# Two matrix products change places, and a bias addition moves from GpSimd to VectorE, in a two-layer graph attention kernel

## The chip, the cores and the metric

The kernel runs on one core of one Trainium2 chip. The metric is the device time of one execution in microseconds (us). The engines are named as in the profile: PE (TensorE, the matrix unit; PEld is its loading of weights), DVE (VectorE), ACT (ScalarE), POOL (GpSimd) and SP (SyncE, which here only issues DMA transfers). Each engine works through its own queue in order; between engines, semaphores hold an instruction back until what it needs is done.

## The reference

There are 64 graphs of 256 nodes with 512 features each, all in float32. Two layers follow each other, each with a residual connection and a normalization over the features:

```python
# layer 0: graph attention, 8 heads of 64
feats = einsum('bnf,hfu->bhnu', X, W)
dense = leaky_relu(e_self[..., :, None] + e_neigh[..., None, :], 0.2)
att = softmax(dense + NEG_BIG * (1 - A))
out = relu(einsum('bhij,bhju->bhiu', att, feats) + b)
x = layernorm(x + out)
# layer 1: attention with an adjacency and a distance term, 8 heads of 64
q, k, v = split(x @ W_qkv)
attn = softmax(q @ k.T / 8) * 0.33 + 0.33 * adj + 0.33 * exp(-adj)     # masked
x = layernorm(x + (attn @ v) @ W_out + b_out)
```

## The kernel before

The nodes of a graph lie in two tiles of 128 rows (`T` = 2) and the features in four chunks of 128 (`C` = 4). The loop runs over the graphs `b`, and one turn of it works on four graphs at once, at different stages: layer 0's attention for graph b (`attend0`), layer 1's projections for b-1 (`proj1`), layer 1's scores for b-1 and its weighting and output for b-2 (`softmax1`, `attend1`), and layer 0's projection for b+1 (`proj0`). A turn is `attention0_beside_projections1(b)` followed by `attention1_beside_projections0(b)`. Both are lists of `do(stage, graph, step, ...)` calls, and `in_order()` ties every instruction to the one issued before it on its engine. So the order of these calls is the order of every engine's queue; no scheduler changes it.

**Seven products for eight.** The projections are multiplied as 2 by 2 blocks in Strassen's manner: seven products p1 to p7, in three PSUM banks. The bank "chain" takes p1, p6, p7 and p4, each added to what lies in the bank; after each of them ACT copies the running sum out (line 301). The bank "alone" takes p2. The bank "pair" takes p5 and then p3. DVE makes the remaining blocks from a bank and one of ACT's copies: `add 11` reads "alone", `add 22` reads "pair" when it holds p5, `add 12` reads "pair" when it holds p5 + p3 (line 304).

```python
BANK = dict(p1="chain", p6="chain", p7="chain", p4="chain", p2="alone", p5="pair", p3="pair")
FIRST = ("p1", "p2", "p5")
COPIES = dict(p1=11, p6=12, p7=22, p4=21)
ADDED = {11: "alone", 22: "pair", 12: "pair"}
```

Two waits follow from this. A product of "chain" waits until ACT has copied the one before it out of the bank, and p3 waits until `add 22` has read the bank. Line 292 holds the matrix products of all three users: `pq_p` (q and k of layer 1), `pv_p` (v of layer 1) and `pf_p` (the features of layer 0, with two columns per head for the attention's logits). All PSUM tiles of this kind rotate through four buffers (`ps_tile`).

**Around the end of the first list.** The second half of v's block ends with p4, the last product of layer 0's attention (`attend0 product 1, 1`, line 539), p3 and `add 12`. Then come `end` (two DVE operations, line 563, which add the input x and sum the rows), the features of the next graph, and between them `squares` of layer 0's normalization on ACT (line 343), the weights of layer 1 (`weights 2` and `weights 3`: two DVE operations each, line 750 times the inverse row sums, line 757 plus the adjacency term), and `norm`. The normalization itself is a chain over three engines: DVE sums (563), POOL takes the mean (338), ACT the squares (343), POOL the factors (350, 353, 354: `shift`), ACT applies them (358). ACT also makes `far`, `at` and `mf` (lines 384, 385, 387) out of the transposed adjacency `adjT` (DVE, line 121) just ahead of the features' first copy. In the second list, the score products `pz` (line 668) use two buffers of their own; ACT's exponentials (line 677) free them.

**The output bias.** `residual` (line 820) adds `b_out`, spread over all rows, to the layer's input `X1[b]` before `sum_up` (line 780) adds the projected attention to it. It has two instructions per graph on POOL (line 822) and stands at the end of the first list, for graph b-2.

**The start of the first list.** Here the products of q and k run between layer 0's weights (`attend0 weights`, line 520, DVE), which begin with `nd` (line 443); `nd` waits for `gb`, a row that is written to DRAM and read back to all partitions. `qk_add 11` and `qk_add 22` are the DVE additions of q and k (line 304).

Of the kernel before, what the change touches and what calls it, by code (L numbers as in the profile page):

```python
# [17 lines left out]
def kernel(  # L18
# [29 lines left out]
    nc = tc.nc  # L48
    P = 128
    NB, N, F = x.shape  # L50
    H, _, U = w0.shape
    T = N // P
# [22 lines left out]
    def ps_tile(shape, name):  # L75

        return psum.tile(shape, FT, tag="mm", name=name, bufs=4)
# [47 lines left out]
    def load(b):  # L125

        XB[b] = io.tile([P, C, N // B, B], FT, tag="xb", name=f"xb_{b}", bufs=1)
        load_blocks(XB[b], x[b])

    def load_adj(b):  # L130
        ADJB[b] = io.tile([P, T, N // B, B], FT, tag="adj", name=f"adj_{b}", bufs=1)
        load_blocks(ADJB[b], adj[b])
        MROW[b] = io.tile([P, N], U8, tag="mask", name=f"mask_{b}", bufs=4)
        nc.sync.dma_start(MROW[b], nodemask[b].partition_broadcast(P))
# [36 lines left out]
    bo_bc = consts.tile([P, F], FT, name="bo_bc")  # L171
# [340 lines left out]
    X1, NORM = {}, {}  # L512
# [231 lines left out]
    def attend1(b):  # L744
        oT = work.tile([P, C, N], FT, tag="oT", name=f"oT_{b}", bufs=1)
        av = {}

        def weights(g):
            p, k = PROBS[b][g], 2 * (g % 2)
            nc.vector.tensor_mul(  # L750
                p,
                p,
                REC[b][:, k : k + 2, g // 2, :]
                .unsqueeze(2)
                .to_broadcast([P, 2, T, N]),
            )
            nc.vector.tensor_add(  # L757
                p, p, CT[b].unsqueeze(1).to_broadcast([P, 2, T, N])
            )

        def values(g):

            if g % 2 == 0:
                av[0] = ps_tile([P, 2, N], f"av1_{b}_{g}")
            for j in range(T):
                for r in range(2):
                    matmul(  # L767
                        av[0][r * U : (r + 1) * U, g % 2, :],
                        V1[b][:, j, 2 * g + r, :],
                        PROBS[b][g][:, r, j, :],  # L770
                        start=(j == 0),
                        stop=(j == T - 1),
                    )
            if g % 2 == 1:
                nc.scalar.copy(oT[:, g - 1 : g + 1, :], av[0])

        def sum_up(po, t):
            if t == 0:
                NORM["l1", b] = LayerNorm(X1[b], b, "l1")
            nc.vector.scalar_tensor_tensor(  # L780
                X1[b][:, t, :],
                po,
                1.0,
                X1[b][:, t, :],
                op0=ALU.mult,
                op1=ALU.add,
                accum_out=NORM["l1", b].sums[:, t : t + 1],
            )
            if t == T - 1:
                NORM["l1", b].mean()  # L790

        PO = {}

        def values_project(g):

            pav = ps_tile([P, N], f"av1_{b}_{g}")
            for j in range(T):
                for r in range(2):
                    matmul(
                        pav[r * U : (r + 1) * U, :],  # L800
                        V1[b][:, j, 2 * g + r, :],
                        PROBS[b][g][:, r, j, :],
                        start=(j == 0),
                        stop=(j == T - 1),
                    )
            nc.scalar.copy(oT[:, g, :], pav)
            if g == 0:
                PO[0] = psum.tile([P, T, F], FT, tag="sc", name=f"po_{b}", bufs=2)
            for t in range(T):
                matmul(  # L810
                    PO[0][:, t, :],
                    oT[:, g, t * P : (t + 1) * P],
                    wo_sb[:, g, :],
                    start=(g == 0),
                    stop=(g == C - 1),
                )
                if g == C - 1:
                    sum_up(PO[0][:, t, :], t)

        def residual():  # L820
            for t in range(T):
                nc.gpsimd.tensor_add(X1[b][:, t, :], X1[b][:, t, :], bo_bc)

        def project(t):
            po = ps_tile([P, F], f"po_{b}_{t}")
            for c in range(C):
                matmul(  # L827
                    po,
                    oT[:, c, t * P : (t + 1) * P],
                    wo_sb[:, c, :],  # L830
                    start=(c == 0),
                    stop=(c == C - 1),
                )
            sum_up(po, t)

        def store():
            NORM.pop(("l1", b)).apply()
            nc.sync.dma_start(out[b].rearrange("(t p) f -> p t f", p=P), X1[b])

        return dict(  # L840
            weights=weights,
            residual=residual,
            values=values,
            values_project=values_project,
            project=project,
            squares=lambda: NORM["l1", b].squares(),
            store=store,
        )
# [3 lines left out]
        proj0=proj0, attend0=attend0, proj1=proj1, softmax1=softmax1, attend1=attend1  # L852
# [3 lines left out]
    def do(stage, b, step, *args):  # L856

        if 0 <= b < NB:
            if (stage, b) not in S:
                S[stage, b] = stages[stage](b)  # L860
            S[stage, b][step](*args)
            in_order()
# [13 lines left out]
    def attention0_beside_projections1(b):  # L876


        do("attend1", b - 3, "squares")
        do("proj1", b - 1, "qk", "p1")  # L880
        do("proj1", b - 1, "qk", "p2")
        if b > 0:
            do("proj0", b, "columns")
        do("proj1", b - 1, "qk", "p6")
        for h in range(HG):
            if b > 0:
                do("proj0", b, "scaled", h)
            do("attend0", b, "weights", h)
        do("attend1", b - 3, "store")
        do("proj1", b - 1, "qk_add", 11)  # L890
        do("proj1", b - 1, "qk", "p5")
        do("proj1", b - 1, "qk", "p7")
        do("proj1", b - 1, "qk_add", 22)
        do("attend0", b, "product", 0, 0)
        if b > 0:
            for h in range(HG, H):
                do("proj0", b, "scaled", h)
        do("proj1", b - 1, "qk", "p4")
        do("attend0", b, "product", 0, 1)
        do("attend1", b - 2, "weights", 0)  # L900
        for h in range(HG, H):
            do("attend0", b, "weights", h)
        do("attend0", b, "norm0", 0, 0)
        do("attend0", b, "norm0", 0, 1)
        do("proj1", b - 1, "qk", "p3")
        do("proj1", b - 1, "qk_add", 12)
        do("attend1", b - 2, "weights", 1)
        do("proj0", b + 1, "xT")
        if b + 2 < NB:
            load(b + 2)  # L910
        do("proj1", b - 1, "values", "p1")
        do("proj1", b - 1, "values", "p2")
        do("proj1", b - 1, "v_add", 11)
        do("proj1", b - 1, "values", "p6")
        do("proj1", b - 1, "values", "p5")
        do("proj1", b - 1, "values", "p7")
        do("proj1", b - 1, "v_add", 22)
        do("proj0", b + 1, "aT")
        if b + 2 < NB:
            load_adj(b + 2)  # L920
        do("attend0", b, "product", 1, 0)
        do("proj1", b - 1, "values", "p4")
        do("proj0", b + 1, "far")
        do("attend0", b, "product", 1, 1)
        do("attend0", b, "norm0", 1, 0)
        do("attend0", b, "norm0", 1, 1)
        do("proj1", b - 1, "values", "p3")
        do("proj1", b - 1, "v_add", 12)
        do("attend0", b, "end")
        do("proj0", b + 1, "product", "p1")  # L930
        do("proj0", b + 1, "product", "p2")
        do("proj0", b + 1, "add", 11)
        do("proj0", b + 1, "product", "p6")
        do("proj0", b + 1, "product", "p5")
        do("proj0", b + 1, "product", "p7")
        do("attend0", b, "squares")
        do("proj0", b + 1, "add", 22)
        do("attend1", b - 2, "weights", 2)
        do("proj0", b + 1, "product", "p4")
        do("attend0", b, "norm")  # L940
        do("proj1", b, "blocks")
        if b + 1 < NB:
            load_rows(b + 1)
        do("proj0", b + 1, "product", "p3")
        do("proj0", b + 1, "add", 12)
        do("attend1", b - 2, "weights", 3)
        do("attend1", b - 2, "residual")

    def attention1_beside_projections0(b):

# [138 lines left out]
```

## Time and profile before

| what | value |
| --- | --- |
| runs shown | 3252.85 us median of 4 (3251.99 to 3253.42) |
| the profiled execution: its time, and its span from first to last instruction | 3252.31 us, 3250.6 us |
| granted PE clock in it | 0.989 |
| busy: PE, DVE, ACT, POOL | 3148.1, 2693.2, 1463.6, 482.9 us |
| one turn of the loop (from one `po` group to the next, 1599.44 to 1648.62) | 49.18 us |
| line 822, POOL, 128x512 | 128 times, 1748 ns mean |
| line 750 / line 757, DVE, 128x1024 | 256 times each, 1217 / 1493 ns mean |
| line 465, DVE, 128x1056, one operand spread over rows | 63 times, 1252 ns mean |

Times are given from the start of the span. In the list of waits, a line names who waited, for whom, the sum in us, how often, and the longest. In the timeline, a line has the start and the length in us, engine, source line, operation, output and inputs, their shapes, the number of instructions merged into it, and in brackets how long the engine had been idle and what ended that. Ends of matrix products are modelled.

### The profile page before, as it was taken

What the parts mean: (1) busy time and instruction counts of PE and PEld (TensorE: products, weight loads), DVE (VectorE), ACT (ScalarE), POOL (GpSimd) and SP (SyncE); (2) the same over time, 40 slices, a digit from 0 to 9 for tenths busy, and PEclk for the clock granted to TensorE, in tenths of its full rate; (3) what the DMA queues carried; (4) which work ended last, traced back from release to release, by engine and by line L of the source; (5) the groups of instructions that cost most, each with busy time, mean ns of one, the idle gap of its engine ahead of it and who ended that gap; (6) DMA issues with size and microseconds to landing.
All of it is one profiled execution on the core that took longest, in us unless ns stands there. A gap on an engine that the chain in (4) does not pass through costs nothing.

```text
span 3250.6 us, 55684 instructions
## 1 busy us (share of the span) xinstructions
PE 3148.1 (97%) x21262; PEld 2491.9 (77%) x21262; DVE 2693.2 (83%) x5088; ACT 1463.6 (45%) x3585; POOL 482.9 (15%) x646
## 2 busy tenths in 40 slices
PE   4999999999999999999999999999999999999997
PEld 4877877877877878878778778778778778778774
DVE  6688888888888888888888888888888888888874
ACT  1344444454444444444444444444444544444442
POOL 0011111111111111111111111111111111111111
PEclk7999999999999999999999999999999999999998
DMA  7244343443443443443443443443444434434421
GB/s 156 68 115 97 102 115 92 106 115 88 108 112 88 108 114 87 109 107 94 112 105 93 115 99 99 115 93 106 115 92 105 115 87 109 111 88 110 112 70 51
DMA packets 764394, 331.87 MB, mean 102 GB/s; under 512 B 696672, under 2 KB 697440, under 8 KB 747744
## 3 DMA queue, kind: packets, MB, share of 16 engines
q1 hardware_dynamic: 764128, 328.30, 39.9%
q8 instruction: 169, 2.77, 0.3%
q14 instruction: 97, 0.79, 0.1%
HBM read 259.80 MB, written 68.16 MB: 101 GB/s over the span
## 4 chain that ended last, share of the span: by engine, by line
PE 95%; ACT 1%; DMA 1%; DVE 1%; SPq 1%; issue 0%; POOL 0%; ACTq 0%; DVEq 0%; POOLq 0%
PE pq_p L292 25%; PE av L539 14%; PE po L827 14%; PE pf_p L292 12%; PE pv_p L292 12%; PE pz L668 8%; PE av L767 7%; PE pd L697 2%; PE pr L82 1%; ACT v L301 1%; SPq L114 0%; PE po L810 0%; DMA hb<-hs 0%; DMA hs<-x 0%; DMA gb<-gs 0%
## 5 line engine op out<-in xcount | busy, mean ns | idle before, releaser
L539 PEld LDWEIGHTS av<-v,pT 128*128 128x128 f32 x4096 | 493.9, 194 | 19.1 <-ACT v L485 12.6
L539 PE MATMUL av<-v,pT 128*128 128x65 f32 x4096 | 491.7, 274 | 12.3 <-ACT v L485 12.3
L292 PE MATMUL pq_p<-hC,wqk_sb 128*128 128x128 f32 x4096 | 482.9, 276 | 0.9 <-ACT qk L301 0.9
L292 PEld LDWEIGHTS pq_p<-hC,wqk_sb 128*128 128x128 f32 x4096 | 467.9, 192 | 2.5 <-ACT qk L301 1.6
L827 PE MATMUL po<-wo_sb,oT 128*128 128x512 f32 x1008 | 460.6, 600 | 0.0
L520 DVE SCALAR_TENSOR_TENSOR pT<-gb,ccol,at 128x256 f32<-128x256 f32 x1024 | 416.9, 480 | 25.0 <-ACT ccol L448 17.8
L757 DVE TENSOR_TENSOR p<-p,ct 128x1024 f32<-128x1024 f32 x256 | 382.2, 1493 | 8.7
L292 PE MATMUL pq_p<-hT,wqk_sb 128*128 128x128 f32 x3072 | 378.0, 280 | 10.4 <-DVE hT L121 9.6
L292 PEld LDWEIGHTS pq_p<-hT,wqk_sb 128*128 128x128 f32 x3072 | 357.1, 194 | 37.1 <-DVE hC L270 25.1
L338 POOL TENSOR_SCALAR nmean_l<-sums_l 128x2 f32<-128x2 f32 x128 | 28.7, 224 | 2349.1 <-DVE x L563 1593.9
L301 ACT COPY v<-pv_p 128x256 f32<-128x256 f32 x256 | 95.3, 372 | 560.8 <-PE pv_p L292 560.8
L827 PEld LDWEIGHTS po<-wo_sb,oT 128*128 128x128 f32 x1008 | 182.0, 190 | 205.0 <-issue 203.6
L750 DVE TENSOR_TENSOR p<-p,rb 128x1024 f32<-128x1024 f32 x256 | 311.5, 1217 | 5.2 <-DMA rb<-rs 5.2
L677 ACT ACTIVATE p<-pz,hide 128x512 f32<-128x512 f32 x512 | 312.2, 708 | 3.3 <-PE pz L668 3.3
L343 ACT ACTIVATE junk<-x,nmean_l 128x512 bf16<-128x512 f32 x256 | 184.9, 722 | 267.8 <-POOL nmean_l L338 263.6
L668 PE MATMUL pz<-qk 64*128 64x256 f32 x2048 | 268.1, 399 | 4.9 <-ACT p L677 4.9
L358 ACT ACTIVATE x<-x,shift_l,rstd_l 128x512 f32<-128x512 f32 x256 | 193.7, 804 | 170.0 <-POOL shift_l L354 170.0
L485 ACT ACTIVATE v<-v 128x64 f32<-128x64 f32 x1024 | 258.6, 339 | 0.0
L767 PE MATMUL av<-p,v 128*64 128x256 f32 x2016 | 249.3, 389 | 2.7 <-DVE p L757 2.7
L668 PEld LDWEIGHTS pz<-qk 64*128 64x128 f32 x2048 | 184.1, 188 | 86.2 <-ACT p L677 46.1
L292 PE MATMUL pv_p<-wv_sb,hC 128*128 128x256 f32 x1024 | 245.5, 382 | 0.0
L292 PE MATMUL pf_p<-wf_sb,xC 128*128 128x264 f32 x1008 | 244.9, 386 | 0.0
(107 smaller groups left out, 4112.4 us busy)
## 6 DMA issues: line engine op xcount, KB each, us to landing
gb<-gs SPq DMA_DIRECT2D x64, 1028.0 KB
rb<-rs SPq DMA_DIRECT2D x64, 1024.0 KB, 4.5
x<-in_x_dram SPq DMA_DIRECT2D x64, 512.0 KB, 4.2
hs<-x SPq DMA_DIRECT2D x64, 512.0 KB
hb<-hs SPq DMA_DIRECT2D x256, 128.0 KB, 3.1
out_dram<-x SPq DMA_DIRECT2D x64, 512.0 KB, 2.9
xb<-in_x_dram SPq DMA_DIRECT2D x252, 128.0 KB, 3.7
adj<-in_adj_dram SPq DMA_DIRECT2D x256, 64.0 KB, 2.9
```

What stands on the lines that cost most here:

```text
L292: matmul(d, lhsT, rhs, start=(p in FIRST and i == 0), stop=(i == len(todo) - 1), skip_group_check=True,)
L343: nc.scalar.activation(junk, self.src[:, t, :], AF.Square, bias=self.nmean[:, t : t + 1], accum_out=self.rstd[:, t : t + 1],)
L358: nc.scalar.activation(self.src[:, t, :], self.src[:, t, :], AF.Identity, bias=self.shift[:, t : t + 1], scale=self.rstd[:, t : t + 1],)
L485: nc.scalar.activation(V0[b][:, t, h, :U], V0[b][:, t, h, :U], AF.Copy, scale=V0[b][:, t, h, U : U + 1],)
L520: nc.vector.scalar_tensor_tensor(pT[h][:, j, :], GB[b][:, h, :N], CCOL[b][:, j, h : h + 1], AT[b][:, j, :], op0=ALU.max, op1=ALU.mult,)
L539: matmul(av[:, k, :], pT[h][:, j, t * P : (t + 1) * P], V0[b][:, j, h, :UA], start=(j == 0), stop=(j == T - 1),)
L668: matmul(pz[:, r, j, :], QK[b][rows, g, 1, j * P : (j + 1) * P], QK[b][rows, g, 0, :], start=True, stop=True,)
L677: nc.scalar.activation(p[:, :, j, :], pz[:, :, j, :], AF.Exp, bias=hide[:, j, b : b + 1], scale=U**-0.5,)
L750: nc.vector.tensor_mul(p, p, REC[b][:, k : k + 2, g // 2, :] .unsqueeze(2) .to_broadcast([P, 2, T, N]),)
L757: nc.vector.tensor_add(p, p, CT[b].unsqueeze(1).to_broadcast([P, 2, T, N]))
L767: matmul(av[0][r * U : (r + 1) * U, g % 2, :], V1[b][:, j, 2 * g + r, :], PROBS[b][g][:, r, j, :], start=(j == 0), stop=(j == T - 1),)
L827: matmul(po, oT[:, c, t * P : (t + 1) * P], wo_sb[:, c, :], start=(c == 0), stop=(c == C - 1),)
```

## The change

`residual` becomes one DVE instruction over both row tiles in place of two POOL instructions. In the first list it moves from the end to the place between `qk_add 11` and `qk_add 22` of the same turn, for the same graph b-2. In the closing list `end()`, its two calls stand where they stood, and run on DVE. At the end of the first list, the features' p1 moves ahead of v's p3, and the features' p2 and `add 11` move behind p7.

```diff
         def residual():
-            for t in range(T):
-                nc.gpsimd.tensor_add(X1[b][:, t, :], X1[b][:, t, :], bo_bc)
+            nc.vector.tensor_add(
+                X1[b], X1[b], bo_bc.unsqueeze(1).to_broadcast([P, T, F])
+            )
...
         do("proj1", b - 1, "qk_add", 11)
         do("proj1", b - 1, "qk", "p5")
         do("proj1", b - 1, "qk", "p7")
+        do("attend1", b - 2, "residual")
         do("proj1", b - 1, "qk_add", 22)
...
         do("attend0", b, "norm0", 1, 1)
+        do("proj0", b + 1, "product", "p1")
         do("proj1", b - 1, "values", "p3")
         do("proj1", b - 1, "v_add", 12)
         do("attend0", b, "end")
-        do("proj0", b + 1, "product", "p1")
-        do("proj0", b + 1, "product", "p2")
-        do("proj0", b + 1, "add", 11)
         do("proj0", b + 1, "product", "p6")
         do("proj0", b + 1, "product", "p5")
         do("proj0", b + 1, "product", "p7")
+        do("proj0", b + 1, "product", "p2")
+        do("proj0", b + 1, "add", 11)
         do("attend0", b, "squares")
         do("proj0", b + 1, "add", 22)
...
         do("attend1", b - 2, "weights", 3)
-        do("attend1", b - 2, "residual")
```

## The prediction

> **What bounds the kernel now.** First the page: which engine sets the end.
>
> ```profile
> PE 95%; ACT 1%; DMA 1%; DVE 1%; SPq 1%; issue 0%; POOL 0%; ACTq 0%; DVEq 0%; POOLq 0%
> ```
>
> PE carries 95% of the chain that ended last. A change gains only where PE waits, and loses only where it makes PE wait. Next the list of waits, for the places that the change touches.
>
> ```profile
> DVE nd L443 <- DMA gb<-gs: 103.6, 64, 3.5
> DVE qk L304 <- ACT qk L301: 77.4, 63, 3.1
> ...
> PEld pz L668 <- ACT p L677: 46.1, 124, 3.4
> ...
> PE pf_p L292 <- ACT v L301: 29.5, 63, 0.5
> ```
>
> The last row is the wait that the new order takes away: p4 of the features waits for ACT's copy of p7. The second is the gap that is to hold the bias addition: DVE waits for the copy ahead of `qk_add 22`, 1.2 us in the mean. The third says that the scores, later in the same turn, wait for ACT too. Third, the timeline of one turn, engine by engine; I count from S = 1628.85, the start of v's p3, just behind layer 0's last attention product.
>
> ```profile
> 1634.85 1.16 PE L292 MATMUL pf_p<-wf_sb,xT 128*128 128x264 f32 x4 [0.47 <-ACT v L301]
> ```
>
> ```profile
> 1629.73 0.39 ACT L387 CAST mf<-mask 128x256 f32<-128x256 uint8 x1
> ...
> 1634.42 0.38 ACT L301 COPY v<-pf_p 128x264 f32<-128x264 f32 x1 [1.40 <-PE pf_p L292]
> ...
> 1639.22 1.52 ACT L358 ACTIVATE x<-x,shift_l,rstd_l 128x512 f32<-128x512 f32 x2 [2.60 <-POOL shift_l L354]
> ```
>
> ```profile
> 1636.44 1.27 POOL L350 TENSOR_SCALAR rstd_l<-rstd_l 128x2 f32<-128x2 f32 x1 [4.34 <-ACT junk L343]
> 1637.79 0.71 POOL L353 TENSOR_TENSOR rstd_l<-rstd_l,mhalf 128x2 f32<-128x2 f32 x1
> 1638.58 0.61 POOL L354 TENSOR_TENSOR shift_l<-nmean_l,rstd_l 128x2 f32<-128x2 f32 x1
> 1639.15 3.48 POOL L822 TENSOR_TENSOR x<-x,bo_bc 128x512 f32<-128x512 f32 x2
> ```
>
> ```profile
> 1637.92 1.22 DVE L750 TENSOR_TENSOR p<-p,rb 128x1024 f32<-128x1024 f32 x1
> 1639.16 2.33 DVE L757 TENSOR_TENSOR p<-p,ct 128x1024 f32<-128x1024 f32 x1
> ```
>
> POOL and DVE stop each other: 354 needs 0.19 us elsewhere (3184.12) and here ends at 1639.19, just as 750 does; 757 takes 2.33 instead of 1.23 while 822 runs, and the next DVE row (393) 1.65 instead of 0.69. ACT's `norm` starts when 354 ends, its exponentials follow without a break, and the fourth of them (end 1643.52) releases the last score product at 1643.58. So the turn's length hangs on 354, not on the features' products alone.
>
> **p1 and p2 move.** *Gain.* PE starts a 128x264 instruction every 0.222 us, so four are 0.89; p4 would start 0.63 earlier without its wait, and its four take 0.99 instead of 0.89 behind it: 0.73 per turn. *New wait.* `add 22` now stands on DVE behind `add 11`, and that behind p2. From S: p1 0.94 (as p3's first instruction behind the attention costs 0.05 more), v's p3 0.86, then p6, p5, p7, p2 at 0.89; p2's last result is out at 5.53 (last start 5.14 and 0.39). `add 11` waits for PE and ACT and starts 0.11 later, as the one such start in the trace, or 0.04, as line 552 does; each addition occupies 0.35. `add 22` runs 5.99 to 6.42, and p3, ready at 6.07, waits for it: 0.33 with the slower start behind a wait. PE keeps 0.73 - 0.33 = 0.40.
>
> **Where that goes.** Weights 2 start 0.35 behind `add 22`, at 6.34 + 0.01; before, at 6.33. `squares` start 0.6 earlier than before, so 350 is ready at 6.7, but DVE's 750 holds it to 7.56. Then 353 falls beside 757 and ends 0.56 behind it (9.39), as in the one place where this happened:
>
> ```profile
> 3160.67 1.69 POOL L353 TENSOR_TENSOR rstd_l<-rstd_l,mhalf 128x2 f32<-128x2 f32 x1
> ```
>
> (757 ended at 3161.80 there.) 354 is ready at 9.47 and is held by 750 of weights 3, as before, to 10.36; before, 10.34. ACT and the last score product then keep their time, and the 0.40 is lost in their wait. Sum: +0.02 per turn, with the short start -0.04; times 62, +1.0 (-2.7 to +1.6).
>
> Here one rule of the Trainium skill ("SBUF — State Buffer", section "SBUF: two separate sides") speaks against the change: of a DVE operation with two SBUF inputs and a POOL operation, whichever starts first keeps the shared ports for its whole length. By it, 353 would hold weights 3's first operation from 9.08 to 9.39, and the sum would be 19 us higher. The trace shows no such hold the other way: 353 began at 1637.79 and ran to 1638.50, and 750 beside it took its usual 1.22 from 1637.92. I go by the row.
>
> **The bias on DVE.** POOL loses 2 x 1.75 us per turn; DVE gets back 1.10 + 0.96 behind 1639, where the same wait for ACT hides it, and pays one 128x1024 operation: 1.22 (line 750), next start after 1.25 (line 465, spread the same way, 1.25). No PE instruction waits for the sum itself until the output projection, half a turn later. But `qk_add 22` and all of DVE's queue to the adjacency transpose stand behind it. The additions' distance in two turns:
>
> ```profile
> 1611.91 0.69 DVE L304 TENSOR_TENSOR qk<-pq_p,qk 128x512 f32<-128x512 f32 x1
> 1614.05 0.69 DVE L304 TENSOR_TENSOR qk<-pq_p,qk 128x512 f32<-128x512 f32 x1 [1.45 <-ACT qk L301]
> ...
> 2548.41 0.69 DVE L304 TENSOR_TENSOR qk<-pq_p,qk 128x512 f32<-128x512 f32 x1
> 2549.61 0.69 DVE L304 TENSOR_TENSOR qk<-pq_p,qk 128x512 f32<-128x512 f32 x1 [0.52 <-ACT qk L301]
> ```
>
> It needs 0.61 + 1.25 = 1.86. In the first turn there are 2.14: it is hidden by the wait for the copy. In the second, `nd` waited 2.85 us for `gb` instead of 1.18, all weights came late, and there are 1.20: `qk_add 22` is 0.66 late. Going through the turns one by one, the distance is under 1.86 in 17 of 62. What is late next: DVE runs without a break (0.14 excepted, a wait of line 520 for PE) to `adjT`; `adjT` releases ACT's `far`, `at` and `mf`; behind `mf` stands the copy of p1; p6 waits for that copy. With p1 0.9 earlier than before, this chain has no slack: `mf` ends at S + 1.2 and p1's result is out at 1.1. In the seven latest turns `adjT` was already 0.49 late against S (2563.28 against 2562.78), which p1's old place hid; with 0.66 more, less 0.10 of slack at p6, each costs 1.05. Two more cost 0.9, two 0.5 and 0.6, two 0.1 to 0.2, four nothing: 7.35 + 1.8 + 1.1 + 0.27 = 10.5. The sums that DVE starts 0.07 earlier without POOL beside it bring `gb` forward by as much: 13 x 0.07 = 0.9 back, 9.6. If p1's copy had slack that I don't see, this is 0; if late turns come as 17 full ones, 18.
>
> **The end.** Behind the last turn, 822 (four, 3184.27 to 3190.21) stretches weights 0: 750 by 0.22, 757 by 0.94 us; q and k's p3 and the values wait behind them. That goes: -1.1. The two additions on DVE now stand ahead of `both`, which is needed only at 3209.9: nothing.
>
> **Sum.** 1.0 + 9.6 - 1.1 = +9.5: the span 3250.6 becomes 3260.1, the execution 3252.31 becomes 3261.8. The median lies 0.5 above that execution: 3262.
>
> **Rivals.** *The removed wait counts* (0.13). For it: 29.5 us is PE's largest wait. If ACT's scores are not held by 354, the 0.40 of 62 turns stay: 3252.9 - 25 + 9.6 - 1.1 = 3236. Against: the score product starts 0.05 behind the fourth exponential, and 354 ends with 750.
>
> *Nothing to measure* (0.30). The late turns find slack, or `gb` comes early enough once POOL is gone: 3252.9 + 1.0 - 1.1 = 3253. For it: 45 of 62 turns have room. Against: the 1.20 of the late turns, and p1 in front of its old cover.
>
> *The addition is too long everywhere* (0.07). Beyond 2.14 + 0.14 - 0.61 = 1.67 us it delays every turn by what is over. If something holds it as 822 held line 393 (0.96), it takes 2.18, 0.51 over in each of 62 turns: 32, or 3285. Against: 750 and 465 at 1.22 and 1.25, and POOL idle at that place.
>
> **The numbers.** The forecast, a little slower by late turns, has 0.50; its own range is 3255 to 3268: from two thirds of the late cost with the short start (3252.9 - 2.7 + 6.4 - 1.1) to half as much again of it with the long one (3252.9 + 1.6 + 14.4 - 1.1). The range 3247 to 3268 leaves out most of the fast rival and of the long addition. This kernel's measurement tells about 0.2% from no change, here 6.5 us (3246 to 3259). A fifth of the forecast falls inside: faster 0.14, same 0.38, slower 0.48.
>
> **What would show it.** Right: PE's row for p4 is gone, PEld waits for DVE at `pf_p` 63 times by some 0.4 us, and PE for ACT there about a dozen times by up to 1 us; `shift` still ends with a 750; PEld's wait for the exponentials grows to 0.5 to 0.8 each; 757 and 393 are back at 1.23 and 0.69. Wrong: turns shorter than 49.1 (the fast rival), PE without waits at p6 (the second), `qk_add 22` late in every turn (the third).

## The result, and the profile after

| | runs | median | range |
| --- | --- | --- | --- |
| before | 59 | 3250.64 us | 3247.78 to 3253.79 |
| changed | 39 | 3256.68 us | 3251.89 to 3261.09 |

The ratio is 1.0019, with a 95% interval of 1.0014 to 1.0023: the change costs 6.0 us, 3.5 us less than the sum said. The interval lies clear of 1, although 6.0 is under the 6.5 us that the prediction took for the least that can be told. The profiled execution of the changed kernel took 3251.89 us (span 3250.1, clock 0.989). It is the fastest of the 39, and it took 0.4 us less than the profiled execution of before. So this pair of traces shows where turns differ, but not the 6.0 us of the medians.

A part of the 6.0 goes with the granted clock of PE. Its mean is 0.9881 over the runs of the changed kernel and 0.9891 over those of the kernel before that ran beside the experiments. Among executions with 0.989 the means are 3254.9 us (11 runs) and 3250.7 us (49 runs), 4.2 apart. Whether the change itself brings the lower clock is not shown.

The page's chain of waits first, the share of each engine in the chain that ended last:

```profile
PE 73%; ACT 10%; POOL 7%; DVE 4%; DMA 3%; issue 2%; SPq 1%; ACTq 0%; DVEq 0%; POOLq 0%
```

Before, PE had 95% of it. ACT and POOL are in it now, although the time is nearly the same: PE waits at another place. The list of waits names that place (who waited, for whom, the sum in us, how often, the longest). Two rows of before, which the prediction did not show:

```profile
ACT x L358 <- POOL shift_l L354: 170.0, 67, 2.8
...
PE pz L668 <- ACT p L677: 4.9, 2, 2.9
```

The changed kernel:

```profile
ACT x L358 <- POOL shift_l L354: 223.5, 67, 3.8
...
DVE nd L443 <- DMA gb<-gs: 88.3, 64, 3.9
...
PEld pz L668 <- ACT p L677: 75.3, 126, 3.4
...
PEld pf_p L292 <- DVE v L304: 29.4, 63, 0.8
...
DVE qk L304 <- ACT qk L301: 21.2, 53, 1.6
PE pz L668 <- ACT p L677: 20.1, 63, 2.9
...
DVE hT L121 <- DMA hb<-hs: 7.4, 9, 2.3
PEld pf_p L292 <- ACT v L301: 5.7, 8, 1.3
...
PE pf_p L292 <- ACT v L301: 2.4, 4, 0.6
```

The wait of p4 for ACT is gone (29.5 us in 63 turns before). What is left, 8 waits of PEld and 4 of PE by up to 0.6 us, stands at p6, once at the start and otherwise in late turns. The prediction expected about a dozen of PE's. In its place are PEld's wait for `add 22` ahead of p3, 63 times, and PE's wait for the exponentials at the scores, up from 4.9 us in 2 turns to 20.1 in 63, with ACT's wait for `shift` up from 170.0 to 223.5. The gap of `qk_add 22` has shrunk from 77.4 to 21.2 us. `hT`, the transposed input of layer 1, had 2 waits for its read-back `hb` before (graphs 0 and 1) and has 9.

The timeline of one turn shows the same as a sequence. Here S = 1826.06 is the start of the features' p1, which now comes first behind layer 0's last attention product:

```profile
1831.70 0.77 DVE L304 TENSOR_TENSOR v<-pf_p,v 128x264 f32<-128x264 f32 x2 [1.98 <-PE pf_p L292]
...
1832.39 1.22 DVE L750 TENSOR_TENSOR p<-p,rb 128x1024 f32<-128x1024 f32 x1
...
1832.76 0.90 POOL L350 TENSOR_SCALAR rstd_l<-rstd_l 128x2 f32<-128x2 f32 x1 [2.73 <-ACT junk L343]
1833.64 1.22 DVE L757 TENSOR_TENSOR p<-p,ct 128x1024 f32<-128x1024 f32 x1
1833.74 1.69 POOL L353 TENSOR_TENSOR rstd_l<-rstd_l,mhalf 128x2 f32<-128x2 f32 x1
...
1835.12 1.21 DVE L750 TENSOR_TENSOR p<-p,rb 128x1024 f32<-128x1024 f32 x1
1835.50 0.88 POOL L354 TENSOR_TENSOR shift_l<-nmean_l,rstd_l 128x2 f32<-128x2 f32 x1
...
1836.42 1.52 ACT L358 ACTIVATE x<-x,shift_l,rstd_l 128x512 f32<-128x512 f32 x2 [3.49 <-POOL shift_l L354]
```

The two additions start at S + 5.64 and 5.99, as forecast. 353 begins 1.26 us earlier from S than in the turn shown of before, and yet 354 ends at S + 10.32: it ends 0.05 us behind weights 3's 750, as it did before. The fourth exponential ends at S + 14.67 in both kernels, and the median turn is 49.177 us, 49.178 before. What PE gained at p4 it gives back at the scores, within 0.01 us.

The rest lies outside the median turn. The span of each profiled execution splits into the time up to the q and k of graph 2, the 60 turns from there on (numbered 1 to 60 below), and what follows:

| us | before | changed | difference |
| --- | --- | --- | --- |
| up to q and k of graph 2 | 176.6 | 173.7 | -2.9 |
| 60 times the median turn | 2950.7 | 2950.6 | 0 |
| what 60 turns take beyond it | 1.9 | 6.5 | +4.6 |
| from there to the end | 121.4 | 119.3 | -2.2 |
| span | 3250.6 | 3250.1 | -0.5 |

Of the 6.5 us, 3.7 lie in six turns with a late `gb` and 2.3 in six turns with a late `hb`, the layer 1 input that is written to DRAM and read back. In before, the 1.9 us lie in seven turns with a late `gb`, at 0.13 to 0.47 each. One of the first kind, turn 19:

```profile
1067.15 0.18 DVE L443 TENSOR_TENSOR nd<-v,gb 128x16 f32<-128x16 f32 x1 [3.19 <-DMA gb<-gs]
...
1071.39 1.22 DVE L821 TENSOR_TENSOR x<-x,bo_bc 128x1024 f32<-128x1024 f32 x1
1072.52 0.69 DVE L304 TENSOR_TENSOR qk<-pq_p,qk 128x512 f32<-128x512 f32 x1
...
1086.17 1.11 PE L292 MATMUL pf_p<-wf_sb,xT 128*128 128x264 f32 x4
1086.18 0.70 DVE L121 STREAM_TRANSPOSE adjT<-adj 128x512 f32<-128x512 f32 x1
...
1088.07 0.39 ACT L387 CAST mf<-mask 128x256 f32<-128x256 uint8 x1
...
1088.36 0.37 ACT L301 COPY v<-pf_p 128x264 f32<-128x264 f32 x1
...
1088.78 2.94 PE L292 MATMUL pf_p<-wf_sb,xC 128*128 128x264 f32 x12 [0.63 <-ACT v L301]
```

`nd` waited 3.19 us, all of DVE came late, and `qk_add 22` stands behind the bias addition with no wait of its own: 1.73 us behind `qk_add 11`. `adjT` starts with p1 (1086.18 against S = 1086.17); `far`, `at` and `mf` follow; the copy of p1 comes at S + 2.19 instead of 1.20, and p6 waits for it. The turn is 1.30 us longer than the median; turns 8 and 33 are 0.89 and 0.95.

### The profile page after: what moved, and what is told of

The parts are those of the page before. It is cut to its first block, busy times and chain, and to the rows that moved or that the text cites. A ratio compares the mean times of both kernels' runs of the same rounds, so it can differ in the third digit from the quotient of the medians.

```text
span 3250.1 us, 55552 instructions
## 1 busy us (share of the span) xinstructions
PE 3156.9 (97%) x21262; PEld 2495.1 (77%) x21262; DVE 2654.6 (82%) x5152; ACT 1460.0 (45%) x3585; POOL 318.0 (10%) x518
## 4 chain that ended last, share of the span: by engine, by line
PE 73%; ACT 10%; POOL 7%; DVE 4%; DMA 3%; issue 2%; SPq 1%; ACTq 0%; DVEq 0%; POOLq 0%
PE pq_p L292 23%; PE av L539 13%; PE po L828 12%; PE pv_p L292 11%; PE pf_p L292 7%; PE pz L668 4%; ACT junk L343 3%; POOL rstd_l L353 3%; ACT x L358 3%; ACT p L677 2%; POOL rstd_l L350 2%; POOL shift_l L354 2%; PE pd L697 2%; DMA gb<-gs 1%; DMA hb<-hs 1%
## 5 line engine op out<-in xcount | busy, mean ns | idle before, releaser
L757 DVE TENSOR_TENSOR p<-p,ct 128x1024 f32<-128x1024 f32 x256 | 313.6, 1225 | 8.7
L668 PE MATMUL pz<-qk 64*128 64x256 f32 x2048 | 273.8, 397 | 21.4 <-ACT p L677 20.1
L358 ACT ACTIVATE x<-x,shift_l,rstd_l 128x512 f32<-128x512 f32 x256 | 193.9, 805 | 223.5 <-POOL shift_l L354 223.5
L292 PE MATMUL pf_p<-wf_sb,xC 128*128 128x264 f32 x1008 | 253.9, 395 | 5.8 <-ACT v L301 2.4
```

What stands on the lines that cost most here:

```text
L292: matmul(d, lhsT, rhs, start=(p in FIRST and i == 0), stop=(i == len(todo) - 1), skip_group_check=True,)
L358: nc.scalar.activation(self.src[:, t, :], self.src[:, t, :], AF.Identity, bias=self.shift[:, t : t + 1], scale=self.rstd[:, t : t + 1],)
L668: matmul(pz[:, r, j, :], QK[b][rows, g, 1, j * P : (j + 1) * P], QK[b][rows, g, 0, :], start=True, stop=True,)
L757: nc.vector.tensor_add(p, p, CT[b].unsqueeze(1).to_broadcast([P, 2, T, N]))
```

## The experiments

All ratios are to the kernel before, which ran beside them on the same chip.

**The two parts alone.** The first kernel is before with the bias addition on DVE ahead of `qk_add 22`, the products unmoved. The second is the changed kernel with the addition back on POOL at its old place.

The first, against before:

```diff
-            for t in range(T):
-                nc.gpsimd.tensor_add(X1[b][:, t, :], X1[b][:, t, :], bo_bc)
+            nc.vector.tensor_add(
+                X1[b], X1[b], bo_bc.unsqueeze(1).to_broadcast([P, T, F])
+            )
...
+        do("attend1", b - 2, "residual")
         do("proj1", b - 1, "qk_add", 22)
...
         do("attend1", b - 2, "weights", 3)
-        do("attend1", b - 2, "residual")
```

The second, against the changed kernel, is the same diff with its signs turned round.

> The kernel before with the bias addition alone moved to VectorE, between qk_add 11 and qk_add 22; the products stand as before. Theory (the change costs time only in turns where gb lands late, and only because p1 has lost its cover): p1's copy has 0.9 us of slack behind mf here, so that a late turn loses 0.3 to 0.5 us instead of 1.05; some +3 us in the loop, -1.1 at the end: 0 to +3 us against before. Rival (the addition on VectorE costs its 0.1 us in every turn wherever p1 stands): +5 to +7 us. Rival (the moved products cost it all): -1 us.

> The changed kernel with the bias addition back on GpSimd at the end of the first list; the products stand as changed. Theory: normal turns keep 49.17 us, since the fourth exponential holds the scores as before; late turns lose up to 0.4 us at p6 (+3 us in all), the first two turns gain 2.9 us: -1 to +1 us against before. Rival (the moved products cost it all): +6 us. Rival (the removed wait counts): -25 us.

Measured: 3252.94 us for the addition alone, ratio 1.0009 [1.0000, 1.0018], and 3253.47 for the moves alone, 1.0010 [1.0002, 1.0019]. Each costs about half of the 6.0, 2.7 and 3.3 us, but both intervals reach almost 3 us to either side, so the halves are rough. The addition alone lies within what was expected, and its median turn is 49.180, so it is not paid in every turn. In its trace six turns with a late `gb` take 0.27 to 0.47 more, and five with a late `hb` 0.29 to 0.58: this second kind comes with the addition, as before and the moves alone have none of it behind graph 1. One further turn takes 1.43 more by another way: v's p3 waits 1.22 for v's `add 22`. The moves alone were expected to cost nothing and cost 3.3: in the trace five turns with a late `gb` take 0.44 to 0.85 us more, without any addition on DVE. p1's old place had hidden a part of what a late `adjT` costs in such turns; its new place doesn't.

**The same change with one place altered.** In the first, the addition stays on DVE but comes just ahead of the output projection, past the late part. In the second, the addition stays where the change put it, and ACT's `far`, `at`, `mf` move behind the copy of p6.

```diff
-        do("attend1", b - 2, "residual")
         do("proj1", b - 1, "qk_add", 22)
...
+        do("attend1", b - 2, "residual")
         do("attend1", b - 2, "project", 0)
```

> The changed kernel with the bias addition on VectorE just ahead of the output projection's first product, where VectorE waits 1.4 us per turn for TensorE, instead of between qk_add 11 and 22. Theory: the lateness of gb is no longer lengthened; -2 to +1 us against before, 6 us under the changed kernel. Rival (VectorE's additional work as such): stays at +6 us.

```diff
-        do("proj0", b + 1, "far")
...
         do("proj0", b + 1, "product", "p6")
+        do("proj0", b + 1, "far")
```

> The changed kernel with ScalarE's far, at and mf issued behind the copy of p6 instead of ahead of the copy of p1; the bias addition stays where the change put it. Theory (adjT, far, mf, copy of p1, p6 is the chain by which a late turn reaches TensorE): p6 never waits for ScalarE by more than 0.1 us, -4 to -1 us against before, 7 to 10 us under the changed kernel. Rival (late turns reach TensorE by another way, as v's p3 behind v_add 22, or the attention products): between +3 and +6 us.

Measured: 3254.06, ratio 1.0010 [1.0002, 1.0019], and 3250.42, ratio 0.9999 [0.9990, 1.0008]. Moving the addition away was expected to give back all 6 us and gives back 2.6, and the two intervals overlap; what stays is about the moves' own cost. Moving `far` brings the time back to that of before, 6.3 us under the changed kernel, with the bias addition still in its gap; 7 to 10 were expected. The waits say the same: PEld's 5.7 us for ACT at `pf_p` in the changed kernel shrink to one wait at the start.

```profile
PEld pf_p L292 <- ACT v L301: 1.3, 1, 1.3
```

The 60 turns take 2.0 us beyond their median, as in before, and turn 8, in which `nd` waits 2.94 for `gb`, is only 0.14 long. So the path of a late `gb` is the one through `adjT`, `far`, `at`, `mf` and the copy of p1 to p6. A late `hb` takes another: four such turns still cost 0.27 to 0.42 each.

**The addition twice.** The changed kernel with the addition issued twice (`b_out` is added twice).

```diff
             nc.vector.tensor_add(
                 X1[b], X1[b], bo_bc.unsqueeze(1).to_broadcast([P, T, F])
             )
+            nc.vector.tensor_add(
+                X1[b], X1[b], bo_bc.unsqueeze(1).to_broadcast([P, T, F])
+            )
```

> The changed kernel with the bias addition on DVE issued twice per graph (b_out is added twice). Theory (qk_add 22 has to wait for whatever the additions ahead of it take beyond the wait for ACT's copy, and DVE's whole queue to the adjacency transpose and p1's copy stands behind it): 0.61 + 2 x 1.25 = 3.1 us against a distance of 2.1, so every turn is late by 0.8 to 0.9 and costs 0.6 to 0.8; a turn of about 49.85, in all 3297 to 3308. Rival (a DVE addition of 1.25 us is hidden in its gap as long as PE doesn't wait for it; late turns have to do with gb alone): a few us more than the changed kernel, 3257 to 3268. Rival (cost in full): 62 x 1.25 = 78 more, 3334.

Measured: 3297.93, ratio 1.0144 [1.0130, 1.0158], as expected. The median turn is 49.785, 0.61 more. ACT's `far` now waits for `adjT` longer in every turn (70.5 us in the changed kernel), and p6 for the copy:

```profile
ACT far L384 <- DVE adjT L121: 121.1, 63, 11.3
...
PE pf_p L292 <- ACT v L301: 29.7, 60, 1.3
```

One addition fits the gap of a normal turn, two don't. `qk_add 22` starts 2.99 us behind `qk_add 11` in the median turn instead of 2.16, and of these 0.83 us 0.61 reach PE by this path.

**gb earlier.** The changed kernel with the logits' `rows` of the next graph ahead of the output projection, and their `bias` earlier on DVE to match.

```diff
+        do("proj0", b + 1, "bias")
         do("softmax1", b - 1, "both", 0)
         do("softmax1", b - 1, "scores", 1)
         do("softmax1", b - 1, "both", 1)
-        do("proj0", b + 1, "bias")
...
+        do("proj0", b + 1, "rows")
         do("attend1", b - 2, "project", 0)
-        do("proj0", b + 1, "rows")
```

> The changed kernel with the logits' bias and rows steps of the next graph ahead of the output projection of layer 1, so that gb is written and read back some 3.5 us earlier. Theory (the loss of the change comes mostly from turns in which gb lands late and the bias addition stands behind the late weights): the turns late by gb vanish (no wait of nd over 4 us any more), 3246 to 3250, that is 6 to 10 under the changed kernel. Rival (the loss is a slower turn, or the layer-1 read-back hb alone): 3254 to 3258. Rival (the earlier rows delay project 0 on PE or add waits on ACT): over 3259.

Measured: 3242.47, ratio 0.9976 [0.9967, 0.9985], 14 under the changed kernel and more than expected. In the median turn the rows on PE come 3.4 us earlier against the next q and k, but the read of `gb` is issued only 0.8 earlier. Still no turn with a late `gb` is left: the longest time from `gb`'s issue to the end of `nd`'s wait (called a flight below) is 6.0 us, where the changed kernel has up to 7.5. Of the rest, 6 us are a shorter median turn, 49.08, which the theory hadn't foreseen. The trace places it on PE: from the start of rows and output projection to the next products (`pd`) it takes 7.40 us instead of 7.50, now that the rows stand ahead of the projection's sixteen products and not between the eighth and the ninth. All other stretches of the turn are the same within 0.01.

**Whether POOL's 354 sets the turn.** The kernel called reordered has weights 2 ahead of `add 11`, weights 3 and values 0 and 1 ahead of p3, the addition ahead of the output projection and `far` behind p6. The diff against the changed kernel, without the last two, which are as above:

```diff
+        do("attend1", b - 2, "weights", 2)
         do("proj0", b + 1, "add", 11)
         do("attend0", b, "squares")
         do("proj0", b + 1, "add", 22)
-        do("attend1", b - 2, "weights", 2)
         do("proj0", b + 1, "product", "p4")
+        do("attend1", b - 2, "weights", 3)
+        do("attend1", b - 2, "values", 0)
+        do("attend1", b - 2, "values", 1)
...
         do("proj0", b + 1, "product", "p3")
         do("proj0", b + 1, "add", 12)
-        do("attend1", b - 2, "weights", 3)
...
-        do("attend1", b - 2, "values", 0)
-        do("attend1", b - 2, "values", 1)
```

The second kernel of this pair is the reordered one with the earlier rows as well.

> The changed kernel with weights 2 ahead of the features' add 11 and weights 3, values 0, values 1, norm and the blocks of layer 1 ahead of p3, add 12 last on DVE; the bias addition just ahead of project 0 of layer 1 and far, at, mf behind the copy of p6. Theory (the 0.4 us that PE keeps in every turn is lost at the score products because POOL's 354 waits for DVE's weights): with the weights earlier, shift and with it the exponentials are ready earlier and PE fills the wait of p3 with values; a turn of about 48.3 us instead of 49.18, about 3196 (3190 to 3203). Rival (PE's own work bounds the turn at this place, 354 is no cause): a turn within 0.15 of 49.18 and 3245 to 3256. Rival (the wait goes elsewhere: values 0 wait for weights 2, or add 12 comes too late for the next turn): over 3256.

> The reordered kernel (weights 2 and 3 and values ahead of p3, bias addition ahead of project 0, far behind p6) with the earlier rows of the next graph as well. Theory: the turn is as short as in the reordered kernel, 48.3 us, and the turns late by gb are gone: 3187 to 3197, 2 to 9 under it. Rival (once the order is changed, nd has slack anyway and late gb costs nothing): within 2 of the reordered kernel. Rival (the rows now stand in front of the shortened chain): slower than it by over 3.

Measured: 3230.61, ratio 0.9938 [0.9924, 0.9951], turn 48.870, and 3225.83, ratio 0.9922 [0.9907, 0.9938], turn 48.767. Both missed their expected times (3196 and 3187 to 3197). The first saved 0.31 us per turn where 0.88 was expected. Its timeline says why (S = 1817.50):

```profile
1827.28 0.68 DVE L393 TENSOR_TENSOR ct<-adjT,far 128x512 f32<-128x512 f32 x1
1827.49 0.52 POOL L354 TENSOR_TENSOR shift_l<-nmean_l,rstd_l 128x2 f32<-128x2 f32 x1
```

354 isn't earlier at all: it ends at S + 10.51, now just behind DVE's 393 (the first of the mask products). Only a copy of ACT (0.59) has moved from behind the normalization to before it, so that the fourth exponential ends 0.30 earlier, at S + 14.37, and the turn is shorter by just that 0.31. The link from the exponentials to the turn holds; the freeing of 354 had not been tried yet.

The next kernel tries it, against the last one: weights 3 behind `add 12`, values 3 behind the scores 2, so that no DVE instruction with two SBUF inputs runs beside POOL's three.

```diff
-        do("attend1", b - 2, "weights", 3)
         do("attend1", b - 2, "values", 0)
...
         do("proj0", b + 1, "add", 12)
...
         do("softmax1", b - 1, "scores", 0)
+        do("attend1", b - 2, "weights", 3)
         do("proj0", b + 1, "shared")
...
-        do("attend1", b - 2, "values", 3)
         do("softmax1", b - 1, "scores", 2)
         do("softmax1", b - 1, "both", 2)
+        do("attend1", b - 2, "values", 3)
```

> The reordered kernel with earlier rows, and in it weights 3 moved behind add 12 and values 3 behind the scores 2, so that no DVE instruction with two SBUF inputs runs while POOL makes the layer 0 factors (350, 353, 354). Theory (354 ends only when DVE's weights let it): 354 ends at about S + 8.5 instead of 10.5, the fourth exponential no longer holds the scores, and the turn becomes 48.55 to 48.65 instead of 48.77: 3212 to 3219. Rival (POOL's factors are as slow without DVE beside them): 354 at S + 10 or later, the turn unchanged, 3224 to 3228. Rival (weights 3 come too late for values 3, or the additions both too late for the row sums): a turn over 48.85, 3231 or more.

Measured: 3257.99, ratio 1.0022 [1.0013, 1.0031]. POOL's timeline there (S = 1829.57):

```profile
1836.27 0.19 POOL L350 TENSOR_SCALAR rstd_l<-rstd_l 128x2 f32<-128x2 f32 x1 [1.83 <-ACT junk L343]
1836.55 0.71 POOL L353 TENSOR_TENSOR rstd_l<-rstd_l,mhalf 128x2 f32<-128x2 f32 x1
1837.33 0.20 POOL L354 TENSOR_TENSOR shift_l<-nmean_l,rstd_l 128x2 f32<-128x2 f32 x1
```

0.19, 0.71 and 0.20 us instead of 0.90, 1.69 and 0.88: 354 ends at S + 7.96, and the scores wait for the exponentials no more. So DVE's weights were what held it. The time is worse all the same. It lies where the last rival had it, something on DVE coming too late, but at an instruction that this rival didn't name: the logits' bias (line 465) stands behind weights 3 and the mask products, about 2.5 us each, and PE waits for it at the logits' rows. The turn is 49.33.

```profile
PEld pr L82 <- DVE v L465: 59.5, 61, 1.0
...
PE pr L82 <- DVE v L465: 46.5, 62, 11.4
```

The last kernel puts that right, with the bias addition where the change has it.

```diff
+        do("attend1", b - 2, "residual")
         do("proj1", b - 1, "qk_add", 22)
...
         do("attend1", b - 2, "weights", 3)
-        do("proj0", b + 1, "shared")
         do("proj0", b + 1, "bias")
...
         do("softmax1", b - 1, "both", 1)
+        do("proj0", b + 1, "shared")
...
-        do("attend1", b - 2, "residual")
         do("attend1", b - 2, "project", 0)
```

> The kernel with weights 3 behind add 12, and in it the layer 0 logits' bias (line 465) right behind weights 3, the mask products (lines 393 to 408) behind both 1, and the output bias addition at the place that the change gave it, ahead of qk_add 22. Theory (in the kernel with weights 3 later, POOL's 354 was free at S + 7.95 and the scores waited no more, but 465 came 2.5 us late and PE waited for it at the logits' rows, 0.6 to 0.8 us a turn): with 465 ahead of the mask products that wait goes, and the addition has room in a gap of 2.8 us; a turn of 48.5 to 48.65, 3209 to 3219. Rival (DVE has no room left in this stretch: the read-back transposes or the row sums come late instead): a turn of 48.8 to 49.3, 3226 to 3256. Rival (the addition ahead of qk_add 22 costs late turns here too): a turn of 48.5 to 48.65, but 3220 to 3227.

Measured: 3218.84, ratio 0.9903 [0.9887, 0.9920]: the fastest of all, 38 us under the changed kernel. The turn is 48.69, a little over the expected 48.65. The 60 turns take 0.02 us beyond their median together, with the addition in front of `qk_add 22`; nothing of the scores' waits is left in the loop; the four of this row lie at the start and at the end.

```profile
PEld pz L668 <- ACT p L677: 7.9, 4, 5.2
```

**Why landings come late.** The trace has a DMA queue of its own for instructions; its row gives packets, MB and share of 16 engines' span:

```profile
q8 instruction: 169, 2.77, 0.3%
```

Each packet has 16,384 bytes, and the trace has 256 PE instructions per packet, matrix products and weight loads counted together. That is why they are taken for PE's instructions here; the trace doesn't name the engine. Two kernels put 32 and 64 unread products at the start of PE's queue, to move the packets in the program; each product counts as two PE instructions.

```diff
     make_identity(nc, ident)
+    pad = ps_tile([P, P], "pad")
+    for _ in range(32):
+        transpose(pad, ident)
```

> The changed kernel with 32 products of the identity with itself at the start of PE's queue, 64 instructions of PE, read by nobody. In the trace of the changed kernel a packet of 16,384 bytes on the instruction queue comes about once per 256 PE instructions; with 64 more in front each comes 64 instructions earlier in the program. Theory (a row gb or the blocks hb land late only where such a packet falls 3 to 5 us behind gb's issue, or 3.2 to 4.5 us behind hb's): moved by 64 instructions, the packets of the changed kernel's trace fall into these windows for gb only at graph 25 and for hb at no graph. So at most two flights of gb over 6.4 us, no wait of hT for hb from graph 5 on, and with the late turns gone 3246 to 3251, 6 to 10 under the changed kernel. Rival (late landings have another cause, the packets only accompany them): hT waits at the same graphs as in the changed kernel (14, 25, 28, 39, 50, 53, 55), and 3255 to 3259.

> The changed kernel with 64 such products, 128 instructions of PE, at the start. Theory (instruction packets in the windows): the packets of the changed kernel's trace, moved by 128 instructions, fall into gb's window at 16 graphs (3, 6, 9, 12, 17, 20, 23, 28, 31, 34, 37, 42, 45, 48, 59, 62) and into hb's at 18 and 43. So hT waits for hb at graphs 18 and 43, late gb at some half of the 16 and hardly elsewhere, and 3255 to 3266, 6 to 16 over the kernel with 32 products. Rival (no such cause): the same graphs late as in the changed kernel, and within 3 of the kernel with 32 products.

Measured: 3263.61, ratio 1.0036 [1.0023, 1.0048], and 3264.76, ratio 1.0041 [1.0028, 1.0055]. The lists of graphs were both missed: the late turns did not vanish. So was the time with 32 products. That with 64 fell into its range, but 1.2 us above the kernel with 32 and not 6 to 16, and only because some 7 us came on top in both ahead of q and k of graph 2, which begin at 180.6 and 180.3 instead of 173.7. No term stood for these. They go at least in part with the granted clock: ahead of that point PE has half its clock for 64.9 and 61.4 us, and for 51.2 in the changed kernel. If PE sets the pace there, that is 6.8 and 5.1 us (an estimate, half of the difference). But the rival falls too. Counting, in each trace, the packets that fall 3.0 to 4.5 us behind the first issue of `hb`, and the waits of `hT` over 0.04 us, from graph 2 on:

| kernel | graphs with such a packet | graphs in which `hT` waited |
| --- | --- | --- |
| before, moves alone | none | none |
| changed | 14, 25, 28, 39, 50, 53 | 14, 25, 28, 39, 50, 53, 55 |
| 32 products | 9, 23, 34, 37, 48, 59, 62 | 9, 23, 34, 37, 48, 59, 62 |
| 64 products | 7, 18, 21, 32, 43, 46, 57 | 7, 21, 32, 40, 43, 46, 57 |

The late graphs move with the packets (graph 9 waited 0.05 us only, and graph 40, which has no packet, 0.04). With `gb` it is the same, less strictly: in the ten kernels with `rows` at their usual place, 59 flights took over 6.4 us (without a packet the median is 5.5 to 5.6), and 58 of these had a packet 3.0 to 5.6 us behind the issue; but most flights with such a packet (204 in all) were not late. So the theory's cause is supported, though how a packet delays a landing is not shown, and its forecast of graphs fell: the expected lists moved the packets by the PE instructions that the trace has on record, with too narrow a window for `gb`, which was evidently too crude. Moving the packets changed which turns were late; for `hb` there are seven, from graph 2 on, in each of the three kernels.

The packets are not the only cause. In the four kernels with `rows` or weights elsewhere in which `hT` still waited (gb earlier, the two reordered ones and the last), it did so 66 times from graph 2 on, and only 11 of these turns had such a packet.

## Why the prediction was right, and where it was off

*The turn: right.* p3's wait for `add 22` was put at 0.33: the first two instructions of p3 start 0.43 and 0.33 behind the ones before them instead of 0.222, 0.32 in all. `shift` stays with the second 750, and the 0.40 are lost at the scores. The sum of +1.0 over 62 turns was 0. The rule of the Trainium skill that spoke against it ("SBUF — State Buffer", "SBUF: two separate sides") is not borne out in this direction: 353 was still running when weights 3's 750 began at 1835.12, and that took 1.21; the profile calls POOL's spans rough. The other direction is plain: POOL's 353 takes 1.69 beside DVE and 0.71 alone.

*The late turns: right in mechanism, mis-sized, and one kind missed.* The path was right link by link, and so was the price of a late turn (1.30, 0.95 and 0.89 against 1.05). What was mis-sized is the term of 9.6, by the step "the distance is under 1.86 in 17 of 62": it took the late turns of one trace as a property of the loop. Before's trace had 8 flights of `gb` over 6.4 us, the changed kernel's 3. The addition also needs less room, 0.60 + 1.13 = 1.73 us. The sum charged all of it to the addition, while the moves alone cost 3.3 us. And the second kind, `hb` landing late ahead of `hT`, was not in the sum: 2.3 us in the profiled execution. With the extra products, the loop of the changed kernel took 7.2 and 10.4 us beyond its median turns in two further profiles. Less the 1.9 that before's loop takes beyond its own, the three profiles give 4.6, 5.2 and 8.5: the 9.6 of the sum lies above all of them.

*The end: right in sign.* -2.2 in this pair of profiles against -1.1. The kernels with the addition on DVE but the loop otherwise as it was need 119.2 to 121.2 us behind the 60 turns, the two with POOL 121.4 and 123.0.

*The start: missed.* No term stood for it; the profiles say -2.9. The granted clock doesn't explain it: PE has half its clock for 51.2 us of this part in both. From layer 0's first attention product to q and k of graph 2, before took 140.7, the changed kernel 138.2 and the moves alone 138.4, so it seems to go with the moved products. It isn't settled, as the kernel with two additions took 140.1. That one differs from the changed kernel by a single addition in this stretch, and has half its clock for 54.6 us.

*The rivals.* "The removed wait counts" fell with the scores' new waits. "Nothing to measure" looks nearest in time (3253 forecast, 3256.68 measured, against 3262), but only because the kernel before ran 2.2 us faster here (3250.64) than in the runs that the prediction started from (3252.85). As a change from before, the rival stands for -0.1, the sum for +9.5, and 6.0 were measured. So the rival fell: late turns do cost, and in the profiles the start and the end pay for some of it. That the `hb` turns, which were not in the sum, made up for a part of what it put too high is luck. "The addition is too long everywhere" fell with the unchanged turn, and the doubled addition shows what it would have looked like.

What stays open: where the 6.0 us of the medians lie, as the profiled execution has none of them; why the packets meet `hb` in no turn of before and of the moves alone, and in five to seven turns of every kernel that has the addition on DVE and `rows` at the usual place with weights in the old order; and why a late packet delays some flights and not others. With `rows` earlier, 56 flights in three kernels had a packet in the same window, and none took over 6.4 us.

## What to carry to other kernels

Before a wait is removed, follow what the engine waits for next: here 0.40 us per turn moved from one place to another, and became time saved in full only when the small POOL operations no longer fell between DVE's large ones. A gap in an in-order queue has the width of its worst turns, and moving a product out of its cover counts as much as filling the gap; with what comes late (`gb`) read 0.8 us earlier, all its late turns were gone. Which turns are late in one trace is not a property of the loop: take their number with a margin, or from several traces.

## What the runs showed of the hardware

Packets of the instruction queue (16,384 bytes, one per 256 PE instructions) are in step with late landings of broadcasts: in the seven kernels with the addition on DVE, `rows` at the usual place and the weights in the old order, `hT` waited 0.05 to 1.0 us in 38 of 41 turns in which such a packet fell 3.0 to 4.5 us behind `hb`'s issue, and 64 or 128 more PE instructions in front of the program moved these turns. Three POOL operations on 128x2 elements take 1.10 us with DVE idle and 3.47 between DVE's 128x1024 operations.
